# Sorting the first eleven row tiles on their own, moving the key extraction behind a product sum, and filling gather slots early in a sparse graph-attention kernel

## The chip, the cores and the metric

The kernel runs on one core of one Trainium2 chip. The metric is device time in microseconds (us) of one execution. TensorE is called PE below, VectorE DVE, ScalarE ACT, GpSimd POOL, and SyncE, which only issues DMAs, SP.

## What is computed

```python
h = jnp.maximum(_layernorm(x, axis=-1), 0.0)          # x: 2708 x 1024
q = h @ W_q.T + b_q ; k = h @ W_k.T + b_k ; v = h @ W_v.T + b_v
z = scale * (q @ k.T)                                  # 2708 x 2708
spare_z = z * adj                                      # adj: 0/1, density 0.0014771
spare_z = jnp.where(spare_z == 0.0, -10000.0, spare_z)
out = jax.nn.softmax(spare_z, axis=1) @ v
return x + jax.nn.relu(out)
```

A row of `adj` has about four ones. So only a few scores of a row count, and the kernel gathers those rows of h instead of forming the 2708 x 2708 matrix.

## The kernel before

**Tiling.** Rows are taken 128 at a time: 22 tiles, the last of 20 rows. The weights of q and k are multiplied into one matrix M at the start (until about 106 us), so that a query row times M is compared with rows of h directly. Tiles 0 to 10 are "early" (`EARLY = 11`), 11 to 21 "late".

**Search.** Each adjacency tile is loaded by SP. ACT sums it (`counted`, step letter p), and DVE finds the positions of the ones in four parts of a row by four `FIND_INDEX8` (`edges`, step letter f; e is p and f together). At the last tile of a batch of four (`BATCHES`), `edges` also turns the positions into sorted keys, by 18 small DVE instructions (lines 322 to 331). 

**Sort.** Rows are sorted by their number of ones, the early and the late rows each among themselves, so that a tile of sorted rows needs few gather slots. `counts` (L567) makes a one-hot table `hot` by counts; `sort` (L589) sums it by two matmuls (`ps_in`, `ps_all`) and makes positions `pos_i`; `put` scatters the 22 tiles of the table `tab` into DRAM by indirect DMAs issued on POOL, and `reload` brings them back in sorted order as `ptab`. The order on POOL is written out by hand in `sort`: late tiles put, early 0 to 3 put, late reload, early 4 and 5 put, first query rows of late tiles gathered (`first_rows`), early 6 to 10 put, early reload.

**Units.** PE's main work is 20 units, and each makes two row tiles times a 1024 x 1024 matrix by seven products of halves instead of eight. Units 0 to 4 are the queries of tiles 0 to 9, in natural order; then `single_query` makes tile 10; units 5 to 9 are the sorted late tiles 11 to 20; units 10 to 19 are outputs, and tile `alone` (11, the last of `order`) follows by itself. `multiply` (L917) runs one unit. Each block is four matmuls of 128x128 by 128x512 (eight instructions in the trace). Its blocks in order are s2, a12, s4, s3, then the next unit's first two (`opened`: a11 and s1), then a22. Between them `after(0)` to `after(6)` issue whatever else belongs there; `steps_at` (L692) lists, by unit and position, the search and normalisation steps. The operands s1 to s4 are DVE differences of transposed halves (L645; s2 and s4 on POOL in units 1 to 3), and the sums `q` (L963, L966) read product banks that PE wants back.

**Attention.** `attention` is a generator that DVE works through between units, from unit 5 on: for each sorted tile `scores` (L782) multiplies gathered rows `g` with the query rows `pq`, ACT makes exponentials (`w`, L798), `sums` (L835) adds the weighted rows into `u`, which goes to `u_dram`. Slots for gathered rows come from `free`: eleven tiles `g` and two parts of M. `fill` issues gathers (L524) while there are wanted rows and free slots. Slots 0 to 7 first hold the weight of v and its differences (`ts_of_wv`, unit 4).

**Order.** DVE keeps program order to the end of the last unit, ACT until unit 5, POOL until `pooled.close()` in `after(2)` of unit 3. PE, SP and the rest are ordered when the program is built, by a scheduler with a model of the times.

Of the kernel before, what the change touches and what calls it, by code (L numbers as in the profile page):

```python
# [18 lines left out]
P = 128  # L19
# [38 lines left out]
def tile_preln_masked_attention(  # L58
# [43 lines left out]
    tab_dram = [dram.tile([N, TW], FT, name=f"tab_dram{i}") for i in range(2)]  # L102
# [167 lines left out]
    def follow(steps):  # L270

        for step in steps.split():
            first, *only = step[1:].split(".")
            first, *last = first.split("-")
            first = int(first)
# [35 lines left out]
    def edges(t):  # L311

        a, n = loaded(t)
        first_t, last_t = next(b for b in BATCHES if b[0] <= t <= b[1])
        G = last_t - first_t + 1
# [3 lines left out]
        for g in range(PARTS):  # L319
            nc.vector.max_index(at[:n, t - first_t, g, :], ones[:n, 0:8], a[:n, g, :])  # L320
        if t == last_t:
# [219 lines left out]
    def put(lo, hi, puts):  # L541

        for t, (t0, n) in tiles_of(lo, hi):
            put = nc.gpsimd.indirect_dma_start(  # L544
                out=tab_dram[lo >= EARLY][:, :], out_offset=bass.IndirectOffsetOnAxis(ap=pos_i[:n, t:t + 1], axis=0),
                in_=tab[:n, t, :], in_offset=None)
            for other in puts:
                tc.declare_no_dep(put.ins, other.ins, reason="rows of a permutation")
            puts.append(put)

    def reload(lo, hi, puts):

        full = min(hi, FULL)
        loads = [nc.gpsimd.dma_start(ptab[:, lo:full, :],
                                     tab_dram[lo >= EARLY][lo * P:full * P, :].rearrange("(t p) w -> p t w", p=P))]
        if hi > FULL:
            loads.append(nc.gpsimd.dma_start(ptab[:REST, FULL, :], tab_dram[1][FULL * P:, :]))
        for load in loads:
            for put in puts:
# [5 lines left out]
    sorting, asked = [], []  # L565

    def counts():  # L567


        s1 = row_tile("sort")  # L570
        s2 = work.tile([P, D], FT, tag="hT", name="hot", bufs=2)
        sorting.extend((s1, s2))
        found = s1[:, 0:NT * SLOTS].rearrange("p (t s) -> p t s", s=SLOTS)
        nc.vector.tensor_scalar(found, keys, 0.0, None, op0=ALU.is_gt)
        nc.vector.tensor_reduce(bad, found, AX.X, ALU.add)
        nc.vector.tensor_copy(tab[:, :, SLOTS + 1:SLOTS + 2], bad.unsqueeze(2))
        nc.vector.tensor_sub(deg, bad, past)
        nc.vector.tensor_scalar_max(deg, deg, -1.0)

        W = ND * NT  # L580
        hot = s2[:, 0:W]
        for lo, hi in parts:
            n = hi - lo
            nc.vector.tensor_tensor(hot[:, ND * lo:ND * hi].rearrange("p (d t) -> p d t", d=ND),
                                    deg[:, lo:hi].unsqueeze(1).to_broadcast([P, ND, n]),
                                    down.unsqueeze(2).to_broadcast([P, ND, n]), op=ALU.is_equal)
        nc.vector.tensor_scalar(tab.bitcast(U32)[:, :, 0:SLOTS], keys, -1.0, float(N), op0=ALU.mult, op1=ALU.add)

    def sort():  # L589

        s1, s2 = sorting
        W = ND * NT
# [12 lines left out]
        for lo, hi in parts:  # L605
            nc.vector.tensor_reduce(deg[:, lo:hi], run[:, ND * lo:ND * hi].rearrange("p (d t) -> p t d", d=ND),
                                    AX.X, ALU.add)
# [19 lines left out]
        with tc.issue_after(back.ins):  # L627
            for t in sorted(owed):
                owe(t)
        return placed  # L630
# [42 lines left out]
    def natural_rows(n):  # L673
# [18 lines left out]
    steps_at = {(0, 0): "s4-5 e9", (0, 1): "r4 +0 +1 +2 f10", (0, 3): "p10 f11", (0, 4): "a4 p11", (0, 5): "h4 +3 s6-7 e12",  # L692
# [6 lines left out]
    def searched():  # L699
# [11 lines left out]
        with tc.issue_after(asked[0].ins):  # L711
            for i in range(8, HIGH):
                nc.gpsimd.memset(slots[i], 0.0)
        assert len(adj_loads) == NT
        free.extend(slots + [M.rearrange("p i j (a c) w -> p i j a (c w)", a=2)[:, 0, 1, a, :] for a in range(2)])
# [200 lines left out]

    def multiply(n, results, after):  # L917
# [20 lines left out]
        if n != FIRST - 1:  # L938
            opened(n + 1)
# [132 lines left out]
    def single_query():  # L1072
# [4 lines left out]
        add_block(X, single[0], M[:, 0, 0])  # L1077
        first = small("p_single")
        nc.scalar.copy(first, X)
# [14 lines left out]
    for n, unit in enumerate(units):  # L1094
# [10 lines left out]
        def after(i):  # L1105
            if (n, i) == (3, 2):
                pooled.close()
                counts()
            if (n, i) == (3, 3):
                with tc.issue_after(products[-1].ins):  # L1110
                    placed.append(sort())
            if (n, i) in ((4, 1), (4, 2)):
                ts_of_wv(2 * i - 2, 2 * i)
            if n == FIRST - 1 and i == 6:
# [31 lines left out]
            if (n, i) == (3, 4):  # L1146
                searched()
            if n == last_q - 1 and i == 4:
# [13 lines left out]
    while alone not in done:  # L1162
        advance(1.0)
# [38 lines left out]
    r, = load_rows(("o", alone))  # L1202
    uT = turned(r, "alone")
    X, Z = banks_for(bp_sb)
    add_block(X, uT[:, 0:4, :], M[:, 0, 0])
    p1 = small("p1")
    nc.scalar.copy(p1, X)
# [190 lines left out]
```

## Time and profile before

| | us |
|---|---|
| runs of the kernel | 671.61, 672.36, 674.16 (median 672.36) |
| the profiled execution's own time | 671.25 |
| its span, first to last instruction | 669.5 |
| PE busy in the span | 653.4 |
| DVE, ACT, POOL busy | 518.4, 266.2, 403.1 |
| DMA bytes, mean rate | 194.29 MB, 290 GB/s |
| first matmul of the M stage | 5.35 |
| first block of unit 0 | 108.59 |
| pair of sort matmuls | 203.57 |
| first score on DVE | 272.05 |
| last matmul ends, about | 660.8 |

Busy time of matmuls is taken from modelled ends, since they are pipelined. So in what follows the distance from the start of one block to the start of the next is used. It is 3.43 us in an undisturbed block of eight instructions, and 0.87 us for eight transposes.

### The profile page before, as it was taken

What the parts mean: (1) busy time and instruction counts of PE and PEld (TensorE: products, weight loads), DVE (VectorE), ACT (ScalarE), POOL (GpSimd) and SP (SyncE); (2) the same over time, 40 slices, a digit from 0 to 9 for tenths busy, and PEclk for the clock granted to TensorE, in tenths of its full rate; (3) what the DMA queues carried; (4) which work ended last, traced back from release to release, by engine and by line L of the source; (5) the groups of instructions that cost most, each with busy time, mean ns of one, the idle gap of its engine ahead of it and who ended that gap; (6) DMA issues with size and microseconds to landing.
All of it is one profiled execution on the core that took longest, in us unless ns stands there. A gap on an engine that the chain in (4) does not pass through costs nothing.

```text
span 669.5 us, 6372 instructions
## 1 busy us (share of the span) xinstructions
PE 653.4 (98%) x1764; PEld 332.4 (50%) x1764; DVE 518.4 (77%) x998; ACT 266.2 (40%) x399; POOL 403.1 (60%) x397
## 2 busy tenths in 40 slices
PE   7999999999999999999999999999999999999994
PEld 4777776444444444444444444444444444444441
DVE  5999879999589402799988899798788989989201
ACT  3467985855844212232242231432332433322220
POOL 2559991585513778676666366574674877872342
PEclk9999999999999999999999999999999999999998
DMA  8997989699566877799999999998997899794653
GB/s 344 407 360 262 368 302 374 235 372 352 204 218 227 279 242 229 270 373 348 326 340 352 403 411 386 293 306 247 333 294 191 235 304 356 212 284 141 175 136 117
DMA packets 62452, 194.29 MB, mean 290 GB/s; under 512 B 9721, under 2 KB 10073, under 8 KB 61514
## 3 DMA queue, kind: packets, MB, share of 16 engines
q0 software_dynamic: 34608, 109.77, 50.0%
q1 hardware_dynamic: 26794, 80.89, 32.5%
q10 hardware_dynamic: 1008, 3.15, 1.2%
q8 instruction: 16, 0.26, 0.2%
q14 instruction: 26, 0.21, 0.1%
HBM read 161.38 MB, written 45.46 MB: 309 GB/s over the span
## 4 chain that ended last, share of the span: by engine, by line
PE 83%; DVE 6%; issue 4%; DMA 3%; POOL 2%; ACT 1%; POOLq 0%; DVEq 0%
PE ps L898 37%; PE psy L898 26%; PE ps_y L397 6%; PE ps_x L397 5%; PE pt L338 4%; PE ps_z L397 4%; DVE junk L782 2%; DVE u L835 2%; DMA g<-h_dram,tab 2%; POOL g L524 1%; DMA out_dram<-y,tab 1%; DVE s L645 1%; DMA wlow<-in_wk_dram 1%; ACT a L641 0%; ACT u L827 0%
## 5 line engine op out<-in xcount | busy, mean ns | idle before, releaser
L524 POOL DMA_INDIRECT g<-h_dram,tab x106 | 129.9, 1226 | 46.7 <-issue 23.4
L898 PE MATMUL psy<-wlow,s 128*128 128x512 f32 x320 | 144.2, 593 | 1.3 <-ACT u L927 1.3
L898 PE MATMUL ps<-M,a 128*128 128x512 f32 x320 | 144.1, 593 | 0.1
L782 DVE SCALAR_TENSOR_TENSOR junk<-g,pq 128x1024 uint8<-128x1024 f32 x94 | 115.1, 1225 | 14.7 <-DMA pq<-q_dram,tab 12.6
L835 DVE SCALAR_TENSOR_TENSOR u<-g,coef,u 128x1024 f32<-128x1024 f32 x78 | 100.0, 1282 | 7.9 <-ACT u L827 4.9
L898 PEld LDWEIGHTS psy<-wlow,s 128*128 128x128 f32 x320 | 59.2, 190 | 69.4 <-issue 66.8
L898 PEld LDWEIGHTS ps<-M,a 128*128 128x128 f32 x320 | 59.3, 190 | 68.0 <-issue 67.2
L320 DVE FIND_INDEX8 at<-ones,adj 128x8 uint32<-128x685 f32 (+1 forms) x88 | 74.4, 865 | 0.0
L898 PE MATMUL psy<-wlow,a 128*128 128x512 f32 x160 | 72.3, 595 | 1.2 <-DVE q L963 0.8
L898 PE MATMUL ps<-wlow,s 128*128 128x512 f32 x160 | 72.1, 593 | 0.8 <-DVE s L645 0.7
L898 PE MATMUL ps<-M,s 128*128 128x512 f32 x160 | 71.9, 592 | 0.0
L981 POOL DMA_INDIRECT y<-in_x_dram,tab x21 | 37.0, 1763 | 49.2 <-ACT y L996 23.1
L309 ACT ACTIVATE sized<-adj 128x2708 uint8<-128x2708 f32 (+1 forms) x22 | 54.2, 2465 | 4.2 <-DMA adj<-in_adj_dram 4.1
L898 PEld LDWEIGHTS psy<-wlow,a 128*128 128x128 f32 x160 | 30.0, 190 | 40.3 <-issue 34.2
L898 PEld LDWEIGHTS ps<-wlow,s 128*128 128x128 f32 x160 | 30.2, 190 | 39.8 <-issue 37.1
L898 PEld LDWEIGHTS ps<-M,s 128*128 128x128 f32 x160 | 30.3, 190 | 37.6 <-issue 37.1
L257 POOL TENSOR_TENSOR hsum<-hsum,x 128x1024 f32<-128x1024 f32 (+1 forms) x17 | 40.3, 2371 | 0.4
L645 DVE TENSOR_TENSOR s<-a,pt 128x512 f32<-128x512 f32 x40 | 25.6, 682 | 17.5 <-ACT a L641 9.2
L641 ACT COPY a<-pt 128x512 f32<-128x512 f32 x60 | 33.2, 593 | 4.9 <-issue 3.3
L544 POOL DMA_INDIRECT tab_dram<-tab,pos_i x22 | 22.6, 1028 | 20.2 <-DVE pos_i L608 13.8
L827 ACT ACTIVATE u<-g,coef 128x1024 f32<-128x1024 f32 x16 | 18.4, 1148 | 34.8 <-DVE coef L826 26.8
L736 POOL DMA_INDIRECT out_dram<-y,tab x21 | 25.1, 1195 | 8.9 <-issue 5.8
(230 smaller groups left out, 871.6 us busy)
## 6 DMA issues: line engine op xcount, KB each, us to landing
adj<-in_adj_dram SPq DMA_DIRECT2D x21, 1354.0 KB
x<-in_x_dram SPq DMA_DIRECT2D x21, 512.0 KB
h_dram<-x POOLq DMA_DIRECT2D x21, 512.0 KB
u_dram<-u POOLq DMA_DIRECT2D x15, 512.0 KB
or<-u_dram SPq DMA_DIRECT2D x15, 512.0 KB
q_late<-q SPq DMA_DIRECT2D x10, 512.0 KB
pq<-q_late POOLq DMA_DIRECT2D x10, 512.0 KB
g<-in_wv_dram SPq DMA_DIRECT2D x16, 256.0 KB
```

The lines of the kernel that those rows point to most:

```text
L257: nc.gpsimd.tensor_add(hsum[:n], hsum[:n], xt[:n])
L309: nc.scalar.activation(sized[:n], a[:n, :, :PW], AF.Abs, accum_out=total[:n, t:t + 1])
L320: nc.vector.max_index(at[:n, t - first_t, g, :], ones[:n, 0:8], a[:n, g, :])
L338: nc.tensor.transpose(pt[:, c, :], xt[:, k * P:(k + 1) * P], ident)
L397: mm = nc.tensor.matmul(bank, a_tile(o + H * a[0], a[1], i), b(o), start=first and o == 0, stop=(o == H - 1), skip_group_check=True)
L524: return nc.gpsimd.indirect_dma_start(out=dst, out_offset=None, in_=src, in_offset=off, bounds_check=N - 1, oob_is_err=False)
L641: nc.scalar.copy(ops[name], bank)
L645: step = (eng or nc.vector).tensor_tensor(ops[name], a, b, op=op)
L782: chained(lambda: nc.vector.scalar_tensor_tensor(junk, g_of[t][s], 1.0, tq[t], op0=ALU.mult, op1=ALU.mult, accum_out=zall[:, t, s:s + 1]))
L835: chained(lambda: nc.vector.scalar_tensor_tensor(u, g_of[t][s], coef[:, at[t][s]:at[t][s] + 1], u, op0=ALU.mult, op1=ALU.add))
L898: mm = nc.tensor.matmul(bank, a[:, c, :], b[:, c, :], start=False, stop=(c == 3), skip_group_check=True)
L981: return nc.gpsimd.indirect_dma_start(out=y[:n], out_offset=None, in_=x, in_offset=off, compute_op=ALU.add)
```

## The change

Five things change.

1. **Search of tile 11.** `edges` is split into `found` (the four index searches, letter i) and `listed` (the keys of a finished batch, letter j). In unit 0 position 3 becomes `p10 i11`, and the keys of the batch 8 to 11 are made at position 4, behind the sum q of the s4 block and behind the operands s1 and s3 of unit 1.
2. **Two sorts.** `counts` and `sort` take a range of tiles. The early range is counted at position (2,1) and sorted at (2,4); the search of tile 19 goes from (2,4) to (2,5), behind the other sum q of unit 2; the early tiles are put and reloaded after it (step w), and POOL's fixed order ends there. The late range is counted and sorted in unit 3, where all 22 tiles were, and `entered` puts and reloads it, gathers the first query rows and adds the owed rows.
3. **Gather slots.** Three tiles are asked for instead of two. The two parts of M and slots 8 to 10 are handed out first, at (4,2); slots 0 to 7 follow where the first entries were filled before, at (4,6). The zeroing of slots 8 to 10 no longer waits for the first query rows.
4. **First block of tile 10.** It goes between s3 and a22 of unit 4 (`between`, `one_started`), where other units have `opened`; it stood behind a22.
5. **Tile `alone`.** Its `u` is loaded and transposed at position 1 of the last unit, and its first block goes ahead of a22 of that unit. Its other three blocks stay at the end.

```diff
+    def put(lo, hi):
+        before_them = puts[lo >= EARLY]
...
-    def counts():
-        s1 = row_tile("sort")
-        s2 = work.tile([P, D], FT, tag="hT", name="hot", bufs=2)
...
+    def counts(lo, hi):
+        n = hi - lo
+        s1, s2 = [work.tile([P, D], FT, tag="hT", name=name, bufs=2) for name in ("sort", "hot")]
...
-        placed = nc.vector.tensor_copy(pos_i, deg)
-        late, early = [], []
-        put(EARLY, NT, late)
-        with tc.issue_after(late[-1].ins):
-            put(0, 4, early)
-        with tc.issue_after(early[-1].ins):
-            back = reload(EARLY, NT, late)
-        with tc.issue_after(back.ins):
-            put(4, 6, early)
-        with tc.issue_after(early[-1].ins):
-            rows = first_rows(0)
+        return nc.vector.tensor_copy(pos_i[:, lo:hi], deg[:, lo:hi])
+
+    def entered():
+        with tc.issue_after(put(EARLY, NT).ins):
+            late = reload(EARLY, NT)
+        with tc.issue_after(late.ins):
+            rows = first_rows(0)
         with tc.issue_after(rows.ins):
             rows = first_rows(1)
-        asked.append(rows)
-        with tc.issue_after(rows.ins):
-            put(6, EARLY, early)
-        with tc.issue_after(early[-1].ins):
-            back = reload(0, EARLY, early)
...
+            elif step == "c":
+                counts(0, EARLY)
+            elif step == "o":
+                sort(0, EARLY)
+            elif step == "w":
+                pooled.close()
+                with tc.issue_after(put(0, EARLY).ins):
+                    back.append(reload(0, EARLY))
             else:
                 if step[0] == "e":
                     counted(first)
-                edges(first)
+                if step[0] != "j":
+                    found(first)
+                if step[0] != "i":
+                    listed(first)
...
-    steps_at = {(0, 0): "s4-5 e9", (0, 1): "r4 +0 +1 +2 f10", (0, 3): "p10 f11", (0, 4): "a4 p11", (0, 5): "h4 +3 s6-7 e12",
+    steps_at = {(0, 0): "s4-5 e9", (0, 1): "r4 +0 +1 +2 f10", (0, 3): "p10 i11", (0, 4): "j11 a4 p11", (0, 5): "h4 +3 s6-7 e12",
...
-                (1, 6): "f16", (2, 1): "f17", (2, 2): "p16 a8", (2, 3): "h8 f18 p17",
-                (2, 4): "s10 f19 p18", (2, 5): "r10", (2, 6): "f20 f21 a10 k10 p19", (3, 2): "p20", (3, 3): "p21"}
+                (1, 6): "f16", (2, 1): "f17 c", (2, 2): "p16 a8", (2, 3): "h8 f18 p17",
+                (2, 4): "o s10 p18", (2, 5): "f19 r10 w", (2, 6): "f20 f21 a10 k10 p19", (3, 2): "p20", (3, 3): "p21"}
...
-        free.extend(slots + [M.rearrange("p i j (a c) w -> p i j a (c w)", a=2)[:, 0, 1, a, :] for a in range(2)])
+        free.extend([M.rearrange("p i j (a c) w -> p i j a (c w)", a=2)[:, 0, 1, a, :] for a in range(2)] + slots[8:])
...
-        for t in order[:2]:
+        for t in order[:3]:
             ask(t)
+        fill()
+        yield 0.0
...
+        free.extend(slots[:8])
         fill()
         yield 0.0
...
+    def between(n):
+        if n == FIRST - 1:
+            single["first"] = one_started(single["banks"], single[0])
+        elif n == len(units) - 1:
+            single["first"] = one_started(single["banks"], single["turned"][:, 0:4, :])
+        else:
+            opened(n + 1)
+
+    def one_started(banks, a):
+        X, Z = banks
+        add_block(X, a, M[:, 0, 0])
+        first = small("p_single")
+        nc.scalar.copy(first, X)
+        return first
...
-        if n != FIRST - 1:
-            opened(n + 1)
+        between(n)
...
             if (n, i) == (3, 2):
-                pooled.close()
-                counts()
+                counts(EARLY, NT)
             if (n, i) == (3, 3):
                 with tc.issue_after(products[-1].ins):
-                    placed.append(sort())
+                    placed.append(sort(EARLY, NT))
+                entered()
...
-            if n == FIRST - 1 and i == 6:
+            if (n, i) == (FIRST - 1, 2):
+                next(stream)
+            if (n, i) == (FIRST - 1, 6):
...
+            if nxt is None and i == 1:
+                while alone not in done:
+                    advance(1.0)
+                r, = load_rows(("o", alone))
+                single["turned"] = turned(r, "alone")
+            if nxt is None and i == 3:
+                single["banks"] = banks_for(bp_sb)
...
-    while alone not in done:
-        advance(1.0)
```

More of the change, by code (lines that the diff above doesn't have):

```diff
@@ L101, in tile_preln_masked_attention @@
     parts = [(0, EARLY), (EARLY, NT)]
-    tab_dram = [dram.tile([N, TW], FT, name=f"tab_dram{i}") for i in range(2)]
+    tab_dram = [dram.tile([size, TW], FT, name=f"tab_dram{i}") for i, size in enumerate((EARLY * P, N - EARLY * P))]
     tail_dram = dram.tile([1, D], FT, name="tail_dram")
@@ L320, in edges, with listed @@
             nc.vector.max_index(at[:n, t - first_t, g, :], ones[:n, 0:8], a[:n, g, :])
+    def listed(t):
+        first_t, last_t = next(b for b in BATCHES if b[0] <= t <= b[1])
+        G = last_t - first_t + 1
+        n = tiles[t][1]
+        at = seen[-1]
         if t == last_t:
@@ L539, in tiles_of @@
         return list(enumerate(tiles))[lo:hi]
-    def put(lo, hi, puts):
+    puts = ([], [])
+    def put(lo, hi):
+        before_them = puts[lo >= EARLY]
         for t, (t0, n) in tiles_of(lo, hi):
@@ L563, in reload, with sort @@
         return loads[-1]
[L565 to L589 removed]
+    sorting, back = [], []
+    def counts(lo, hi):
+        n = hi - lo
+        s1, s2 = [work.tile([P, D], FT, tag="hT", name=name, bufs=2) for name in ("sort", "hot")]
+        sorting[:] = s1, s2
+        found = s1[:, 0:n * SLOTS].rearrange("p (t s) -> p t s", s=SLOTS)
+        nc.vector.tensor_scalar(found, keys[:, lo:hi], 0.0, None, op0=ALU.is_gt)
+        nc.vector.tensor_reduce(bad[:, lo:hi], found, AX.X, ALU.add)
+        nc.vector.tensor_copy(tab[:, lo:hi, SLOTS + 1:SLOTS + 2], bad[:, lo:hi].unsqueeze(2))
+        nc.vector.tensor_sub(deg[:, lo:hi], bad[:, lo:hi], past[:, lo:hi])
+        nc.vector.tensor_scalar_max(deg[:, lo:hi], deg[:, lo:hi], -1.0)
+        nc.vector.tensor_tensor(s2[:, 0:ND * n].rearrange("p (d t) -> p d t", d=ND),
+                                deg[:, lo:hi].unsqueeze(1).to_broadcast([P, ND, n]),
+                                down.unsqueeze(2).to_broadcast([P, ND, n]), op=ALU.is_equal)
+        nc.vector.tensor_scalar(tab.bitcast(U32)[:, lo:hi, 0:SLOTS], keys[:, lo:hi], -1.0, float(N), op0=ALU.mult, op1=ALU.add)
+    def sort(lo, hi):
         s1, s2 = sorting
[L592 removed]
+        W = ND * (hi - lo)
         hot = s2[:, 0:W]
@@ L1201, in tile_preln_masked_attention @@
     tail(NT - 1)
[L1202 to L1207, printed above, removed]
+    uT, (X, Z), p1 = single["turned"], single["banks"], single["first"]
     add_block(Z, uT[:, 0:4, :], T[:, 0])
```

37 lines of the change are left out of this document (15 added, 22 removed).

## The prediction

> **What bounds the kernel now.** I read the page's busy times first, then the waits of PE, then PE's timeline, and last what stood on the waited-for engine.
>
> ```profile
> PE 653.4 (98%) x1764; PEld 332.4 (50%) x1764; DVE 518.4 (77%) x998; ACT 266.2 (40%) x399; POOL 403.1 (60%) x397
> ```
>
> PE is busy from end to end, at a mean granted clock of 0.997. The change takes no product away, so it can win only PE's gaps. At the ends nothing of it acts: M starts as before, and from the last matmul's end (660.8) a DVE sum, a scatter and the closing waits run to 669.5. The gaps between are few:
>
> ```profile
> PE psy L898 <- ACT u L927: 1.3, 1, 1.3
> PE psy L898 <- DVE q L963: 0.8, 1, 0.8
> PE ps L898 <- DVE s L645: 0.7, 1, 0.7
> ...
> PE ps_in L595 <- DVE hot L584: 0.5, 1, 0.5
> ```
>
> Ends of matmuls are modelled, so I size each gap by starts (PE's timeline: start, us, instructions):
>
> ```profile
> 130.39 3.60 PE L898 MATMUL ps<-M,a 128*128 128x512 f32 x8
> 134.71 3.70 PE L898 MATMUL ps<-wlow,s 128*128 128x512 f32 x8 [0.73 <-DVE s L645]
> ...
> 186.38 3.60 PE L898 MATMUL ps<-wlow,s 128*128 128x512 f32 x8
> 190.74 3.70 PE L898 MATMUL psy<-wlow,a 128*128 128x512 f32 x8 [0.76 <-DVE q L963]
> ...
> 199.46 3.60 PE L898 MATMUL ps<-M,a 128*128 128x512 f32 x8
> 203.57 0.90 PE L595 MATMUL ps_in<-hot,before 128*128 128x396 f32 x2 [0.52 <-DVE hot L584]
> ...
> 271.64 3.60 PE L898 MATMUL ps<-M,s 128*128 128x512 f32 x8
> 276.58 3.70 PE L898 MATMUL psy<-wlow,s 128*128 128x512 f32 x8 [1.35 <-ACT u L927]
> 280.12 3.60 PE L898 MATMUL ps<-M,a 128*128 128x512 f32 x8
> 283.80 3.70 PE L898 MATMUL ps<-wlow,s 128*128 128x512 f32 x8
> 287.57 3.70 PE L898 MATMUL psy<-wlow,a 128*128 128x512 f32 x8
> ```
>
> An undisturbed block takes 3.43 from start to start, and the first block behind a gap 0.11 more. So the gaps cost: A at 134.71, 4.32 - 3.43 + 0.11 = 1.0; B at 190.74, 4.36 - 3.43 + 0.11 = 1.04; C at 203.57, 4.11 - 3.43 = 0.68; D from 276.58 to 287.57, 1.51 + 0.11 + 0.25 + 0.34 + 0.11 = 2.32; E, a wait for the sum L991 at 573.53, 0.62. Sum 5.7: the most that this change can win.
>
> **Keys behind the sum (gap A).** DVE has no idle time from 106 to 153. Behind tile 11's search it makes the keys of a batch, 130.19 to 133.37 (3.2), then the sum q (L966), and only at 133.98 the operands s1 and s3 that PE waits for. Afterwards s1 and s3 follow the sum directly, at 130.75; their inputs are there (ACT's copy of a22 ends at 128.15). PE's s1 block then starts at 133.82 without a wait. The keys now stand ahead of the sum L963, which ends at 135.8 as before, since the work ahead of it is the same; its taker, a22, starts at 137.25. **Gain 1.0.**
>
> **Early sort in unit 2 (gap B).** DVE's sum for a22 stood behind tile 19's search and a batch of keys (183.4 to 190.0). Both move behind it. The early `counts` adds seven DVE instructions: before, over 22 tiles, they took 0.34, 0.52, 0.19, 0.17, 0.18, 0.64 and 0.34 (2.4 in all); over 11 tiles about 1.6. They lie in DVE's idle time 168.6 to 173.1 (a wait for ACT, 4.58); without this cover they would cost unit 2's operands 1.6. The early `sort` adds seven more: 0.56, 0.98, 0.57, 0.57, 0.57, 0.46, 0.18 at double width, some 2.6 at this one. It waits for its two matmuls, and behind it on DVE wait tile 10's statistics (1.5), the sum (0.6), tile 19. PE, 1.0 earlier by gap A, starts the matmuls at 178.5 and s3 at 179.3; DVE is through with the sort near 182.5 and with the sum near 184.7. PE wants it at 189.6. So gap B goes (1.04) and a pair of matmuls is paid: 203.57 to 204.98 was 1.41 for 396 columns, so about 0.7 for 198. **Gain 0.35.**
>
> **Late sort (gap C).** DVE's search of tiles 20 and 21 began at 192.15, after 1.47 of waiting for the adjacency load. The moved batch ends near 191.3, so it stays under that wait. The load goes out when ACT has summed tile 17, and ACT may be up to 1.0 earlier; I take 0.5. From 201.35 `hot` took 2.08; eleven tiles should take 1.4. `hot` is ready at 201.35 - 0.5 + 1.4 = 202.25, the pair starts at 202.4 and takes 0.7: unit 3 goes on at 203.1 instead of 204.98. This is **1.9 for A, B and C together** (with the load at its old time 1.4, a full 1.0 earlier 2.3).
>
> **Early gathers (gap D).** DVE's first score waited to 272.05:
>
> ```profile
> 272.05 1.22 DVE L782 SCALAR_TENSOR_TENSOR junk<-g,pq 128x1024 uint8<-128x1024 f32 x1 [12.62 <-DMA pq<-q_dram,tab]
> ```
>
> The early table was reloaded last (issued at 251.63), six gathers and two qr rows went ahead of pq (265.95) on POOL's queue, and the DMA engines were 0.9 busy from 258 on, at 1.6 to 1.8 per 512 KB. ACT, in the order laid down for it, held the exponentials (idle 10.3 for L782) ahead of the copy u (L927) that PE needed. Now eleven puts (1.3 apart, 14.3) and the reload run from about 187 to 205 on a POOL that idled until 210.97 but for one store; late puts follow from 208 to 222 and query rows are gathered near 229 instead of 237.81. Five gathers, 2.6 MB, can go before 255, where the DMA share was 0.66 and 0.26 in the last two stretches of 5. Tile 10's store (255.81, some 2 earlier now) then frees pq: it lands between 260 and 264 against 270 on the moved scale. Gap D needs the first three scores done by 272 there, that is, a start before 268. **Gain 2.3**, bounds 0 and 2.32.
>
> **Tile `alone`.** PE has as many blocks as before. Its transposes (0.87) only filled the wait of a22 for the sum L991 (642.51 to 643.42), which its first block fills now. **Gain 0**, and a risk: the transposes are asked for at the last unit's start, 628.64.
>
> ```profile
> 622.31 0.60 POOL L844 DMA_DIRECT2D u_dram<-u  x1
> ...
> 628.36 0.34 SPq L1048 DMA_DIRECT2D or<-u_dram  x1
> 630.00:631.00 1.00, 1.00 (x4) 0.49 (x3) 0.00 (x0) 0.06 (x1) 1.00 (x1) 1.00 0.91 373
> ```
>
> The store takes 5.45 from 622.91 to release its load, whose bytes move until about 631.2 (the last row is a stretch of 1 us: DMA share 0.91, 373 GB/s). All of it shifts with PE. Transposes put first would wait 2.6; behind the s2 block (632.07), nothing. [...]
>
> Gap E stays: DVE meets PE at 511.36 (it waits 1.28 for it) and is late again by its own work at 573, so it shifts with PE (bounds 0 to 0.62).
>
> **Sum.** 1.9 + 2.3 = **4.2**, taken from the profiled execution of 671.25: 667.0 (span 665.3). The median of the runs, 672.36, lies 1.1 above it; on that scale **668.2**, with 1.4 to 2.3 plus 2.0 to 2.9 (a little of E) giving 667.2 to 669.0.
>
> **Rivals.**
> - *The load of `alone` is late.* PE takes the transposes first, waits 2.6 and pays 0.3 around it: gain 1.3, 671.1. For it: they stand first in program order. Against: before, the scheduler put them into a gap, and a modelled late load would again.
> - *The pq wait stays.* POOL sends the second five gathers ahead of pq, 5 x 1.8 = 9 of queue, and the first score starts at 270: gain 1.9 alone, 670.5. For it: that is what POOL did before. Against: idle DMA time before 255.
> - *The early sort stalls DVE: slower.* If its matmuls are put behind the blocks a11 and s1 that unit 2 opens instead of ahead of s3, DVE stands until 190.3; sort, statistics and sum end at 195.0, a22 starts at 195.1 instead of 189.6, tiles 19 to 21 end near 210.6, the late pair starts at 212.1 and unit 3 goes on at 212.8, 7.9 late; less D, 5.5: 677.9. It decides once the pair is later than about 186. For it: nothing ties these matmuls to a place. Against: their input is ready at 170 and they come first in program order.
>
> **How the numbers follow.** The forecast has 0.47, the late load 0.2, the pq wait 0.12, the slow sort 0.15, and 0.06 is for a wait that I don't see. Half a per cent, 3.4, is about what a measurement of this kernel can tell from no change; the line lies at 669.0. Faster: 0.47 and a little of the rest, 0.5. Within: late load and pq wait, 0.32. Slower: 0.18. The range 666.0 to 672.2 takes in both middle cases, leaving the slow sort out.
>
> **What would show it.** In PE's waits the lines of L645, of L963 and of L927 are gone, and that of `hot` is at most 0.5; the early `pos_i` is written near 183; the first score starts before 266 with `pq` gathered by 259; the last unit's s2 block starts 3.43 after a22's. A wait of PE for `or` or its copies, or for the early `ps_in`, makes the prediction wrong; so does a DVE wait of over 3 us in unit 2.

## The result, and the profile after

The changed kernel takes **678.58 us** (median of 11 runs, 674.90 to 680.21) against 672.36 before (11 runs, 670.75 to 675.90). The ratio is **1.0081, 95% interval 1.0059 to 1.0104**: slower by 0.8 per cent, where the prediction had 668.2 and a range of 666.0 to 672.2. The profiled execution took 678.58, its span 676.8, 7.3 more than the 669.5 before.

PE's waits in the changed kernel (who waited for whom: us in total, times, longest):

```profile
PE psy L904 <- DVE q L985: 2.7, 1, 2.7
PE pt L355 <- DMA or<-u_dram: 2.6, 1, 2.6
PE ps_in L611 <- ACT a L645: 2.0, 1, 2.0
...
PE psy L904 <- DVE p L1013: 0.4, 1, 0.4
```

The waits that were to go are gone from their places: the one for s1 and s3 (L645 before), the one for the sum in unit 2 (L963 before) and the one for the copy u (L927 before). Three longer ones have come. One is for the same sum (L985 now), but in unit 1. One is for `or`, the row of `alone`. One stands ahead of the late pair, where at most 0.5 was to be left. PE's timeline shows where (start, us, instructions):

```profile
130.01 3.60 PE L904 MATMUL ps<-M,a 128*128 128x512 f32 x8
133.45 3.60 PE L904 MATMUL ps<-wlow,s 128*128 128x512 f32 x8
137.12 3.70 PE L904 MATMUL psy<-wlow,a 128*128 128x512 f32 x8
...
165.86 5.40 PE L904 MATMUL psy<-wlow,a 128*128 128x512 f32 x8 [2.69 <-DVE q L985]
171.09 1.04 PE L355 MATMUL pt<-ident,x 128*128 128x128 f32 x8
...
183.15 0.50 PE L611 MATMUL ps_in<-hot,before 128*128 128x198 f32 x2
183.48 0.50 PE L613 MATMUL ps_all<-hot,ones 128*128 128x198 f32 x2
183.82 3.60 PE L904 MATMUL psy<-wlow,s 128*128 128x512 f32 x8
...
208.36 0.57 PE L611 MATMUL ps_in<-hot,before 128*128 128x198 f32 x2 [2.03 <-ACT a L645]
...
633.87 1.70 PE L355 MATMUL pt<-ident,or 128*128 128x128 f32 x8 [2.57 <-DMA or<-u_dram]
635.36 3.83 PE L904 MATMUL psy<-wlow,s 128*128 128x512 f32 x6
639.03 3.60 PE L904 MATMUL ps<-M,a 128*128 128x512 f32 x8
```

The reader should set each start against the same block before. That gives a running balance of how late PE is:

| reached | after - before | what came in between |
|---|---|---|
| first block of unit 0 | -0.38 | differs before the change acts |
| a22 of unit 0 | -1.13 | gap A gone |
| first transposes behind unit 1's a22 | +3.62 | waits 2.69 for the sum, then the block takes 1.7 too long |
| s3 of unit 2 | +4.30 | the early pair, 0.67 |
| a22 of unit 2 | +3.38 | gap B gone |
| s4 of unit 3 | +4.12 | waits 2.03 ahead of the late pair |
| a22 of unit 5 (287.57 before) | +1.73 | gap D gone |
| last unit, a12 (632.07 before) | +6.96 | waits 2.57 for the row of `alone`, six matmuls and transposes too slow |
| last blocks of `alone` (653.72 before) | +6.13 | its transposes are no longer here |
| end of the span | +7.3 | the end behind PE is 1.2 longer |

Behind two of the waits PE also ran slower. By stretches of 1 us (PE, PEld, DVE, ACT, POOL busy; then the granted clock, DMA share, GB/s):

```profile
165.00:166.00 1.00, 0.14 (x1) 0.14 (x2) 0.98 (x4) 0.00 (x0) 0.00 (x0) 1.00 0.98 357
166.00:167.00 1.00, 1.00 (x2) 0.38 (x3) 1.00 (x3) 0.00 (x0) 0.00 (x0) 0.75 0.99 385
167.00:168.00 1.00, 1.00 (x3) 0.35 (x2) 1.00 (x3) 0.00 (x0) 0.00 (x0) 0.50 0.56 222
168.00:169.00 1.00, 1.00 (x3) 0.48 (x2) 1.00 (x3) 0.00 (x0) 0.00 (x0) 0.50 0.08 33
169.00:170.00 1.00, 1.00 (x3) 0.48 (x2) 1.00 (x5) 0.00 (x0) 0.00 (x0) 0.54 0.03 14
```

The clock is at half for 0.50 + 1 + 1 + 0.92 = 3.42 us, which costs 1.7. From 634 to 638 it is the same (0.57, 0.50, 0.50, 0.73: 3.40 at half). Whether the clock falls differs from run to run of one kernel, and the times with it: six of twelve runs of alone_keys_again (below) took 669.14 to 669.59 at a mean granted clock of 0.996, the other six 671.14 to 671.87 at 0.993 to 0.995. The store of the row of `alone` and the load that PE waits for there, from the queues of POOL and SP in the changed kernel:

```profile
623.86 0.60 POOL L847 DMA_DIRECT2D u_dram<-u  x1
...
630.08 0.34 SPq L1070 DMA_DIRECT2D or<-u_dram  x1
```

On DVE two things had changed their length, and one load came late (changed kernel, DVE's timeline):

```profile
131.56 0.98 DVE L342 TENSOR_TENSOR cand<-first,at 128x128 f32<-128x128 f32 x1
132.58 1.31 DVE L343 SCALAR_TENSOR_TENSOR cand<-at,cand 128x128 f32<-128x128 uint32 x1
...
149.52 0.09 DVE L330 MATCH_VALUE_LOAD at<-ones,adj 128x8 f32 x1 [2.52 <-DMA adj<-in_adj_dram]
...
184.42 2.51 DVE L617 TENSOR_TENSOR_SCAN sort<-sort 128x198 f32<-128x198 f32 x1
```

The same instructions in the kernel before:

```profile
130.19 0.29 DVE L325 TENSOR_TENSOR cand<-first,at 128x128 f32<-128x128 f32 x1
130.52 0.29 DVE L326 SCALAR_TENSOR_TENSOR cand<-at,cand 128x128 f32<-128x128 uint32 x1
...
206.72 0.98 DVE L601 TENSOR_TENSOR_SCAN sort<-sort 128x396 f32<-128x396 f32 x1
```

The two key instructions took 0.29 each before. The scan took 0.98 for 396 columns and now takes 2.51 for half as many. Tile 14's adjacency was searched without a wait in the trace of the kernel before. POOL's timeline in the changed kernel, beside the key instructions:

```profile
131.13 1.27 POOL L649 TENSOR_TENSOR s<-s,a 128x512 f32<-128x512 f32 x1 [1.32 <-DVE s L649]
132.47 1.26 POOL L649 TENSOR_TENSOR s<-a,s 128x512 f32<-128x512 f32 x1
133.69 0.66 POOL L255 DMA_DIRECT2D h_dram<-x  x1
134.37 2.37 POOL L257 TENSOR_TENSOR hsum<-hsum,x 128x1024 f32<-128x1024 f32 x1
136.67 0.58 POOL L255 DMA_DIRECT2D h_dram<-x  x1
```

And in the kernel before:

```profile
134.74 1.27 POOL L645 TENSOR_TENSOR s<-s,a 128x512 f32<-128x512 f32 x1 [4.61 <-DVE s L645]
...
137.30 0.66 POOL L255 DMA_DIRECT2D h_dram<-x  x1
...
140.28 0.57 POOL L255 DMA_DIRECT2D h_dram<-x  x1
```

There POOL idled until 134.74, waiting for s1 and s3, and its two stores of h went out at 137.30 and 140.28. So the moved keys now run beside the very work that they used to hold back, and the stores (512 KB each) start 3.6 us earlier.

### The profile page after: what moved, and what is told of

It is laid out like the page before. It is cut to its first block, busy times and chain, and to the rows that moved or that the text cites. A ratio compares the mean times of both kernels' runs of the same rounds, so it can differ in the third digit from the quotient of the medians.

```text
span 676.8 us, 6390 instructions
## 1 busy us (share of the span) xinstructions
PE 655.5 (97%) x1768; PEld 334.8 (49%) x1768; DVE 525.7 (78%) x1010; ACT 266.3 (39%) x399; POOL 402.1 (59%) x397
## 4 chain that ended last, share of the span: by engine, by line
PE 74%; DVE 10%; DMA 7%; issue 4%; ACT 3%; POOL 1%; POOLq 0%; ACTq 0%; SPq 0%; DVEq 0%
PE ps L904 32%; PE psy L904 23%; PE ps_y L414 6%; PE ps_x L414 4%; PE ps_z L414 4%; PE pt L355 4%; DMA adj<-in_adj_dram 3%; DVE u L838 2%; DVE at L330 2%; DVE junk L785 1%; DVE s L649 1%; DMA y<-in_x_dram,tab 1%; ACT sized L320 1%; DMA u_dram<-u 1%; DMA out_dram<-y,tab 1%
## 5 line engine op out<-in xcount | busy, mean ns | idle before, releaser
L541 POOL DMA_INDIRECT g<-h_dram,tab x104 | 124.6, 1198 | 51.3 <-issue 22.8
L785 DVE SCALAR_TENSOR_TENSOR junk<-g,pq 128x1024 uint8<-128x1024 f32 x92 | 112.6, 1223 | 2.0
L904 PE MATMUL psy<-wlow,a 128*128 128x512 f32 x160 | 73.9, 606 | 3.1 <-DVE q L985 2.7
L649 DVE TENSOR_TENSOR s<-a,pt 128x512 f32<-128x512 f32 x40 | 25.6, 680 | 17.2 <-ACT a L645 9.7
L543 POOL DMA_INDIRECT pq<-q_dram,tab x11 | 15.5, 1411 | 33.2 <-DVE junk L785 21.2
L645 ACT COPY a<-pt 128x512 f32<-128x512 f32 x60 | 33.2, 593 | 4.2 <-PE pt L355 4.2
L541 POOL DMA_INDIRECT M<-h_dram,tab x20 | 25.9, 1293 | 11.1 <-issue 4.9
```

The lines of the kernel that those rows point to most:

```text
L541: return nc.gpsimd.indirect_dma_start(out=dst, out_offset=None, in_=src, in_offset=off, bounds_check=N - 1, oob_is_err=False)
L645: nc.scalar.copy(ops[name], bank)
L649: step = (eng or nc.vector).tensor_tensor(ops[name], a, b, op=op)
L785: chained(lambda: nc.vector.scalar_tensor_tensor(junk, g_of[t][s], 1.0, tq[t], op0=ALU.mult, op1=ALU.mult, accum_out=zall[:, t, s:s + 1]))
L904: mm = nc.tensor.matmul(bank, a[:, c, :], b[:, c, :], start=False, stop=(c == 3), skip_group_check=True)
```

## The experiments

Ratios are to the kernel before on the same chip, with 95% intervals. The letters of the steps in the edits, beside those named above: s is the statistics of a tile on DVE, r the eight small POOL instructions that make its scale, a the scaling on ACT, h the stores of two tiles of h and their adds into `hsum` on POOL, k the stores alone, with the adds left owed, and + such an owed add. Dots in the code stand for lines or steps that are not shown.

### Which parts cost

**alone_at_end**: tile `alone` put back to the end, the rest of the change kept.

```diff
-            if nxt is None and i == 1:
...
-                r, = load_rows(("o", alone))
-                single["turned"] = turned(r, "alone")
...
-            single["first"] = one_started(single["banks"], single["turned"][:, 0:4, :])
...
```

> The changed kernel with tile alone left at the end (load, transposes and first block behind the last unit, as before). Theory: in the changed kernel's trace the last unit loses 4.5 us on PE (2.6 of waiting for the load of alone, 1.75 of matmuls at a lower granted clock behind that wait, some transposes), and 1.2 more pass between the last matmul and the end, since the last unit's results reach POOL later. So this kernel is 5.0 to 5.9 us faster than the changed one, near 673, and its granted clock in the last unit is 1.0. Rival: the wait is paid anyway, because PE then waits for the sum L991 in the same unit; the gain is under 1.5 us.

672.39 (669.44 to 674.18), ratio 0.9994 [0.9977, 1.0010]. The early start of `alone` costs 6.2 by the medians (5.8 by the ratios).

**keys_back**: the keys of tile 11's batch back to position (0, 3).

```diff
-    ... (0, 3): "p10 i11", (0, 4): "j11 a4 p11", ...
+    ... (0, 3): "p10 f11", (0, 4): "a4 p11", ...
```

> The changed kernel with the keys of tiles 8 to 11 made in their old place, ahead of the sum q. Theory 1: moving them let POOL store normalised rows 3.6 us earlier and SP ask for x and adjacency tiles 3 us earlier, and that traffic made adjacency tile 14 land 4 us late; here tile 14's search has no wait, a22 of unit 1 starts within 0.5 us of its place in the kernel before, gap A (1.0 us) is back, and the kernel is 3 to 4 us faster than the changed one. Theory 2: the late landing is chance of one execution (the DMA rate was 277 to 337 GB/s around 130 us against 393 to 428); here it comes or stays away as it likes, and over all runs the kernel is 1 us slower than the changed one or the same.

675.89 (673.89 to 676.90), ratio 1.0049 [1.0031, 1.0067]: 2.7 below the changed kernel by the medians, 2.2 by the ratios, where theory 1 had put 3 to 4. Gap A is back (a wait of 1.2 for s L649), and PE's wait in unit 1 is gone. DVE still waits 2.16 for tile 14's adjacency, against theory 1, but its search starts at 147.42 instead of 149.52.

**r10_first**: the eight POOL instructions of r10 ahead of the early puts, which the prediction had assumed.

```diff
...
-                with tc.issue_after(put(0, EARLY).ins):
+                with tc.issue_after(rooted[-1].ins):
+                    last_put = put(0, EARLY)
+                with tc.issue_after(last_put.ins):
...
```

> The changed kernel with the eleven early puts tied behind the eight small POOL instructions of tile 10's scale (r10). In the changed kernel POOL took them in turn with the puts, so they ended at 203.6 us instead of about 192, ACT's step for tile 10 waited 5.3 us and held the copies behind it, and ps_in waited until 208.36. Theory 1: the one-hot table of the late sort was ready at 208.22 by DVE's own lateness, so the late ps_in starts no earlier: a gain under 0.4 us. Theory 2: ACT was what held it: the wait of 2.0 us goes, gain 1.5 to 2.1 us.

677.22 (673.67 to 679.46), ratio 1.0065 [1.0041, 1.0090]. The wait ahead of the late pair is 2.1 as before and only names another releaser, `hot` instead of the copy behind a10. DVE held it too.

**alone_keys**: both undone.

> The changed kernel without the early alone tile and without the moved keys. If the two losses are independent, its gain over the changed kernel is the sum of the two single ones: 8 to 10 us if tile 14's lateness comes from the moved keys (near 669.5, faster than the kernel before by 3), 4 to 5 us if that is chance.

669.47 (669.14 to 671.33), ratio 0.9956 [0.9939, 0.9972]. What is left of the change, the two sorts and the early gathers, gains. A repeat on another chip (alone_keys_again) gave 670.37, 0.9966 [0.9949, 0.9983].

### Tile alone

**alone_later**: the changed kernel; the load stays at position 1 of the last unit, the transposes are asked for at position 4.

```diff
-                r, = load_rows(("o", alone))
-                single["turned"] = turned(r, "alone")
+                single["rows"], = load_rows(("o", alone))
+            if nxt is None and i == 4:
+                single["turned"] = turned(single["rows"], "alone")
```

> The changed kernel, but in the last unit the transposes of tile alone's row are asked for behind the fifth product (i = 4) instead of the second; the load stays where it is. It splits the 6.2 us that tile alone cost into the wait for its row and the rest. Theory 1 (the wait): the changed kernel lost 2.57 waiting for `or`, and the six matmuls behind it took 3.83 where 6/8 of 3.43 is 2.57; without the wait the last unit's blocks start 3.43 apart and the time is 3 to 5 us below the changed kernel's 678.6, 674 to 675.5; the late results of the last unit on POOL's queue (1.2 at the end) stay. Theory 2 (it is the queue at the end, since the first block of alone stands ahead of the last unit's results): no more than 1.5 below the changed kernel.

673.04 (669.84 to 674.45), ratio 1.0008 [0.9990, 1.0025]: 5.5 below the changed kernel by the medians, 4.9 by the ratios. PE's timeline of it:

```profile
635.97 3.60 PE L904 MATMUL ps<-M,s 128*128 128x512 f32 x8
639.40 1.04 PE L355 MATMUL pt<-ident,or 128*128 128x128 f32 x8
640.28 3.60 PE L904 MATMUL psy<-wlow,s 128*128 128x512 f32 x8
```

The same transposes, three blocks later, wait for nothing and take 1.04, and the block behind them takes its 3.60. **later_keys** (the same with the keys put back) tells whether the queue at the end costs as well:

> The changed kernel with the keys put back and tile alone's transposes asked for behind the fifth product: all the rest of the change stays. The prediction gave tile alone's early start a gain of 0 if its load doesn't hold PE. Theory 1 (the wait was all there is to it): within 0.7 of alone_keys. Theory 2 (GpSimd's queue at the end costs 1.2, since the last unit's results come one block later): 0.8 to 1.5 above alone_keys.

670.31 (669.93 to 672.48), ratio 0.9979 [0.9961, 0.9998], against 670.37, ratio 0.9966, for alone_keys on the same chip: equal by the medians, 0.9 slower by the ratios. So the wait and its clock were most of it. The early start of `alone` wins nothing, and a cost of up to 0.9 at the end (theory 2) is not ruled out.

### The late pair

**alone_keys_r10** (alone_keys with r10 first, the edit above):

> Tile alone and the keys put back (669.5 so far), and on GpSimd's queue the root of tile 10 (r10) ahead of the early puts, as the prediction assumed. Theory 1 (DVE's own lateness holds the late pair of matmuls): the wait of 2.1 for the copy behind a10 becomes one for `hot`, about as long, time within 1 of 669.5. Theory 2 (r10 between the puts holds it): the wait falls below 0.7 and the time is 667.5 to 668.5.

670.83 (668.87 to 672.03), ratio 0.9974 [0.9957, 0.9991]; PE's wait ahead of the late pair is 2.07, as with r10 between the puts. That is theory 1's wait; the time is 1.4 above the first median of alone_keys and 0.5 above the second, where at most 1 was put. **alone_keys_k8** moves two POOL adds away from beside the early sort's scan; **alone_keys_s10** moves the scan instead, by putting tile 10's statistics ahead of the sort:

```diff
-    ... (2, 3): "h8 f18 p17", ...
+    ... (2, 3): "k8 f18 p17", ...      # alone_keys_k8: the stores, the adds later
-    ... (2, 4): "o s10 p18", ...
+    ... (2, 4): "s10 o p18", ...       # alone_keys_s10
```

> alone_keys with one edit: GpSimd's two adds of tiles 8 and 9 into hsum, one of which runs beside the early sort's scan, are made later, among the gathers. Theory 1 (the scan is slow because GpSimd adds beside it): the scan takes 0.6 instead of 2.5, `hot` of the late tiles is 1.9 earlier; since r10 still stands between the puts, ACT's copy behind a10 holds the late pair as before and the wait stays 1.5 to 2.0, so the time is within 1 of alone_keys. Theory 2 (a scan of 198 columns is slow by itself here): it stays at 2.5.

> alone_keys with one edit: in unit 2 tile 10's statistics stand ahead of the early sort on DVE. They have one SBUF input and took 1.28 beside GpSimd before; so the scan starts 1.5 later, overlaps GpSimd's add by 0.6 instead of 2.1, and r10 is ready before the puts, which follow it in GpSimd's order. Theory 1 (scan beside the add, and r10 between the puts, together hold the late pair): scan 1.0 to 1.4, `hot` ready 1 to 1.5 earlier, the wait of 2.05 falls below 1.2, no drop of the granted clock behind it, time 1 to 3 below alone_keys. Theory 2 (something else, such as the adjacency load, holds DVE): the wait stays at 1.8 or more and the time within 0.5.

668.00 (667.27 to 669.29), ratio 0.9933 [0.9907, 0.9959], and 668.03 (667.50 to 671.30), 0.9938 [0.9916, 0.9959]. From DVE's and PE's timelines of alone_keys_k8:

```profile
180.60 0.57 DVE L617 TENSOR_TENSOR_SCAN sort<-sort 128x198 f32<-128x198 f32 x1
...
202.31 0.37 DVE L600 TENSOR_TENSOR hot<-deg,down 128x198 f32<-128x198 f32 x1
```

```profile
202.82 0.57 PE L611 MATMUL ps_in<-hot,before 128*128 128x198 f32 x2 [0.31 <-DVE hot L600]
```

PE's timeline of alone_keys:

```profile
204.90 0.62 PE L611 MATMUL ps_in<-hot,before 128*128 128x198 f32 x2 [2.05 <-ACT a L645]
```

The scan is back at 0.57 and the late pair starts at 202.82 with a wait of 0.31, where alone_keys had 204.90 and 2.05. With the scan moved it overlaps POOL's add by some 0.8 and takes 1.19, and the wait is 0.47. The wait that I thought r10 shared in is the scan's alone: in alone_keys_k8 r10 still stands between the puts. My expectation of "within 1 of alone_keys" was wrong there: it is 2.4 faster on the same chip. Part of this is PE's clock. In alone_keys it was 0.50 for 3.42 us behind this wait, and the block of 3.60 behind the pair took 4.96; in the repeat that block took 5.01, in the traces of these two kernels 3.60.

### The moved keys

**b_keys**: the kernel before with the moved keys alone.

> The kernel before with the moved keys alone (batch made behind the sum L963's place: tile 11 only searched at (0, 3), keys at (0, 4)). Forecast in the prediction: gain 1.0, gap A gone and nothing else. Theory 1 (the keys slow down beside GpSimd): the two instructions with two SBUF inputs that take 0.29 each before now take about 1.0 and 1.3 beside GpSimd's s2 and s4, the sum for a22 of unit 1 is late again and PE waits there 1 to 3 us: time 0 to +3 against before. Theory 2 (the loss needs the other parts, the earlier stores or the early sort): gap A gone, no wait in unit 1, time 0.5 to 1.0 below before.

673.45 (671.30 to 678.70), ratio 1.0035 [1.0013, 1.0057]. The loss needs no other part of the change. PE waits 2.02 in unit 1, as theory 1 had it; whether its cause holds is for the next kernels. **alone_keys5**: `alone` at the end, and the batch one step later, behind the sum for a22.

> Tile alone put back to the end, and the moved keys one step later still: at the head of (0, 5), behind the sum for a22 and past GpSimd's s2 and s4. Against alone_at_end (keys at (0, 4), 672.4) and alone_keys (keys where they were, 669.5). Theory 1 (GpSimd beside it is what the move costs): the two instructions take 0.29 each again, gap A stays away, PE's wait for the sum in unit 1 is below 0.5, time 668 to 669.5. Theory 2 (any keys behind a22's sum push tile 12's search and the adjacency loads back, and unit 1's sum with them): the wait in unit 1 is 1 us or more and the time 671 to 673.

673.02 (670.99 to 674.82), ratio 1.0011 [0.9992, 1.0031], with a wait in unit 1 of 3.6. These are the numbers of theory 2, but POOL was still beside the keys (busy for 3.90 of the 4 us from 132 to 136; the two instructions took 0.39 and 1.31), so theory 1 wasn't put to the test. In its trace the stores of h go out at 133.74 and 136.73, and DVE waits 1.38 and 2.40 for the adjacency of tiles 13 and 14. The next kernels stand on **mended_base** (alone_keys_k8 once more), which repeats at 668.24, ratio 0.9951 [0.9937, 0.9964]. **keys4_k8** has the keys where the change puts them, **keys11_k8** ahead of tile 14's search, and **all_mended** is keys11_k8 with the early start of `alone` as in alone_later.

```diff
-    ... (0, 3): "p10 f11", (0, 4): "a4 p11", ...     (1, 1): "f14", ...       # mended_base
+    ... (0, 3): "p10 i11", (0, 4): "j11 a4 p11", ... (1, 1): "f14", ...       # keys4_k8
+    ... (0, 3): "p10 i11", (0, 4): "a4 p11", ...     (1, 1): "j11 f14", ...   # keys11_k8
```

> mended_base with the keys at the place that the change gives them, behind the sum and beside GpSimd's s2 and s4. Both theories: the wait for the sum in unit 1 is back, 1.4 to 2.7, and the time 1.5 to 3.5 above mended_base.

> mended_base with the keys later still, ahead of tile 14's search (step (1, 1)), when GpSimd has made s2, s4 and two of its three adds. Theory 1 (GpSimd beside the keys is the cost): the first instruction takes at most 0.6 and the second 0.29, the batch lies where DVE would wait for the adjacency load, gap A is gone, PE's wait for the sum of unit 1 is below 0.5, time 0 to 1 below mended_base. Theory 2 (a later batch takes DVE's slack, wherever it stands): the wait in unit 1 is 1 or more and the time is 1 or more above mended_base.

> The whole change with three faults undone: keys ahead of tile 14's search, the two adds moved from beside the scan, tile alone's transposes asked for behind the last unit's fifth product (its early start stays). Expected the time of keys11_k8 within 0.8, and 9 to 12 below the changed kernel's 678.6.

keys4_k8: 670.80, ratio 0.9980 [0.9965, 0.9995], 2.6 above mended_base with a wait of 2.35 in unit 1, as expected. keys11_k8: 671.84, 1.0004 [0.9991, 1.0018]. all_mended: 671.20, 0.9998 [0.9984, 1.0012], close to keys11_k8, but 7.4 below the changed kernel where 9 to 12 was expected. DVE's timeline of keys11_k8, then PE's:

```profile
143.59 0.09 DVE L330 MATCH_VALUE_LOAD at<-ones,adj 128x8 f32 x1 [4.88 <-DMA adj<-in_adj_dram]
...
146.97 0.27 DVE L342 TENSOR_TENSOR cand<-first,at 128x128 f32<-128x128 f32 x1
147.28 0.29 DVE L343 SCALAR_TENSOR_TENSOR cand<-at,cand 128x128 f32<-128x128 uint32 x1
```

```profile
166.38 5.40 PE L904 MATMUL psy<-wlow,a 128*128 128x512 f32 x8 [3.04 <-DVE q L983]
```

My theory fell here, and the time and the wait are those of theory 2. The instructions are short again, POOL is not beside them, and PE waits longer: DVE stands 4.88 for tile 13's adjacency load, and the batch comes behind that. What all kernels with gap A closed share is a POOL that is 3 us ahead. It then issues its two stores of h, and frees the buffer for the next x load, 3 us earlier, into DMA engines that are full (share 0.96 to 1.04 in each 4 us from 132 to 148 in mended_base, keys4_k8 and keys11_k8). Two kernels delay one of these each, from keys4_k8:

```diff
-    ... (0, 5): "h4 +3 s6-7 e12", (0, 6): "r6 f13", ...
+    ... (0, 5): "+3 s6-7 e12",    (0, 6): "r6 h4 f13", ...   # keys4_h4: the stores later
+    ... (0, 5): "h4 s6-7 e12",    (0, 6): "r6 +3 f13", ...   # keys4_3late: the x load later
```

> keys4_k8 with GpSimd's two stores of h in unit 0 (and their adds) moved behind the add of an owed tile and behind r6: the stores go out near 143 and 146 instead of 134.2 and 137.2; the x load behind that add goes out earlier still, near 137 instead of 142.6. Theory 1 (the earlier stores delay the adjacency load): tile 14's search starts at 147.5 or before, PE's wait in unit 1 falls from 2.4 to below 0.8, time 667.5 to 669.5. Theory 2 (the earlier x and adjacency loads delay it): the search starts at 149.5 or later, the wait stays at 2 or more, time 670.5 or more.

> keys4_k8 with the add of the owed tile moved behind r6 instead: the stores stay at 134.2 and 137.2, the x load and tile 15's adjacency load go out near 145 to 146, as in the kernel before. Theory 1 (the earlier stores): tile 14's search starts at 149.5 or later and the wait in unit 1 stays at 2 or more, time 670.5 or more. Theory 2 (the earlier x and adjacency loads): the search starts at 147.5 or before, the wait is below 0.8, time 667.5 to 669.5.

**keys4_h4: 666.73** (666.00 to 669.30), ratio **0.9928 [0.9910, 0.9946]**, the best of all. keys4_3late: 671.05 (667.84 to 672.63), 0.9979 [0.9963, 0.9995]. PE's waits of keys4_h4, its POOL timeline, and the start of tile 14's search on DVE; then the same start in keys4_3late, keys4_k8 and mended_base:

```profile
PE psy L904 <- DVE p L1011: 0.4, 1, 0.4
PE psy L904 <- DVE q L983: 0.3, 1, 0.3
```

```profile
142.93 0.66 POOL L255 DMA_DIRECT2D h_dram<-x  x1 [0.30 <-issue]
...
145.92 0.58 POOL L255 DMA_DIRECT2D h_dram<-x  x1
```

```profile
146.45 0.09 DVE L330 MATCH_VALUE_LOAD at<-ones,adj 128x8 f32 x1
```

```profile
150.45 0.09 DVE L330 MATCH_VALUE_LOAD at<-ones,adj 128x8 f32 x1 [3.04 <-DMA adj<-in_adj_dram]
```

```profile
149.72 0.09 DVE L330 MATCH_VALUE_LOAD at<-ones,adj 128x8 f32 x1 [2.58 <-DMA adj<-in_adj_dram]
```

```profile
147.07 0.09 DVE L330 MATCH_VALUE_LOAD at<-ones,adj 128x8 f32 x1 [1.72 <-DMA adj<-in_adj_dram]
```

With the stores 9 us later DVE waits for no adjacency load (tile 14's search ends at 149.84, when s1 begins). And that although the x load, free at 136.06, now stands ahead of tile 14's load on SP's queue, so that this goes out at 136.56 instead of 133.28. The 0.3 left is unit 0's. With the x load late and the stores early the wait is 3.04 and PE's 2.80. Of the two, the stores are the cause; how the DMA engines share their time between the queues the traces don't show. The two key instructions still take 0.98 and 1.31 in keys4_h4, and that costs no more than the 0.3. So neither theory 1 of keys11_k8 (POOL beside the keys) nor its theory 2 (a later batch takes DVE's slack, wherever it stands) is the main cost.

One trace can't size the delay. When the load of tile 14 lands differs by 2 us between traces with the keys in their old place: it is there by 145.29 in the kernel before and at 147.42 in keys_back. The kernel before, alone_keys and alone_keys_r10 search tile 14 without a wait, keys_back waits 2.16 and mended_base 1.72, and PE waits in unit 1 in none of them. The latest of these five starts that search at 147.42, the earliest of the eight with the keys at (0, 4) or (0, 5) and the first store before 135 at 148.35 (alone_later). The cost is read from the run times: 0.9979 with the early stores and 0.9928 with the late ones, on one chip. No run delays the stores with the keys in their old place, so what late stores would win by themselves is open.

## Why the prediction was wrong

**Keys behind the sum: 1.0 was to be gained, 1.6 to 2.9 was lost** (by the medians: b_keys against the kernel before 1.6, keys4_k8 against mended_base 2.6, the changed kernel against keys_back 2.7, alone_at_end against alone_keys 2.9). Gap A went, but a22 of unit 0 starts only 0.75 earlier against unit 0's first block: the sum that was to end at 135.8 ended at 137.07, behind the longer key instructions. The step that failed is "the work ahead of it is the same" and with it the list of what the move releases. I followed PE's side of s1 and s3 only. POOL waits for them too, and behind them stand its DMAs: the h stores went out 3.6 earlier, tile 14's adjacency came late, and DVE, which had idled 1.18 in unit 1 before, was late for the sum of unit 1, where PE waited 2.69. The longer key instructions are a second slip, with little price (0.3 in keys4_h4).

**Early sort.** Gap B is gone, and the pair costs 0.67 where 0.7 was put. It starts at 183.15, directly ahead of s3, so the rival of the stalled sort is out. Mis-sized was "some 2.6" for DVE: in alone_keys it is 4.8 (180.53 to 185.30), because the scan takes 2.52 where half of 0.98 was put; in alone_keys_k8, without POOL beside the scan, it is 2.8 (180.20 to 183.03).

**Late sort.** `hot` at 202.25 and the pair at 202.4 were worked out; the changed kernel, 3.4 late by then, has a wait of 2.0. The scan had taken 2 us of the DVE time on which `hot` depends. In alone_keys_k8 the pair starts at 202.82, so the step's working holds once the scan's time does. That r10 would go ahead of the puts was also wrong, and made no difference.

**Early gathers.** Gap D is gone and 2.2 of 2.3 are won (PE is 3.93 late at the start of unit 5's first product block, 272.13, and 1.73 at its a22). pq landed later than I put it: POOL issued its gather at 266.44, once tile 10's store had landed, and the first score started at 270.79, 266.9 without PE's 3.9. So the sign that I had set, a start before 266, was missed, and the bound that decided, a start before 268, held by 1.1.

**Tile `alone`.** Its row in the list of rivals came true: the wait is 2.57 where 2.6 was worked out from the store and load of before. The store was issued at 623.86, the load followed at 630.08. The sign that was to make the prediction wrong, a wait of PE for `or`, is in the trace. What failed is the argument against this rival, that the scheduler would put the transposes into a gap: it put them behind the first quarter of the s2 block, with the load still under way. What times its model gave them the record doesn't show. And the price was short: 2.6 + 0.3 became 4.9 to 6.2. Of the rest 1.7 is the clock, which fell to half for 3.4 us behind the wait, and up to 1.2 the longer end behind PE.

**Gap E** stayed (0.4), as said. **The sum**: 4.2 of gain was close to what the parts are worth where nothing is held up. alone_keys_k8 gains 3.9 on its chip without the moved keys, and keys4_h4 gains 5.2 with them. Part of the latter is luck: in its trace 0.6 of the 5.2 stands already at unit 0's first block (107.96 against 108.59), ahead of anything that the change touches, which leaves some 4.6. The loss lies in three side effects: the load of `alone` (about 6), the stores (about 3) and the scan (about 2, in part through the clock).

## What to carry to other kernels

When a step moves off the bottleneck's path, list what it releases on every other engine, DMAs too, and ask which transfer shares the DMA engines with them; here a store that nobody waited for decided the time of a load (tile 14's search at 149.72 with the stores early, in keys4_k8, and at 146.45 with them late, in keys4_h4). Price an instruction by who runs beside it at its new place: here the two key instructions and the scan on DVE lasted until POOL's operand or add was done (0.29 became 0.98 to 1.36, 0.57 became 2.51). Work whose input comes from a late load should be asked for behind work that covers the load, since an order by modelled times need not do it.

## What was not expected of the hardware

**A wait can cost more than its length.** In the units PE's clock was 0.50 for 3.40 to 3.42 us behind the waits of 2.05 (alone_keys), 2.57 and 2.69 (the changed kernel), and 1.00 behind those of 2.03 (the changed kernel's late pair) and 2.72 (r10_first). For the other waits the blocks behind them tell. Behind 3.04 (keys11_k8) and 3.56 (alone_keys5) the block took 5.40 and 5.39, as behind the 2.69. Behind 2.05 (b_keys), 2.80 (keys4_3late), and 1.75 (all_mended) or less it took no more than 3.70, and behind 2.51 (r10_first) six matmuls took 2.74, where the changed kernel's took 3.83. So waits of 2.0 to 2.8 went either way, two of 2.05 among them; what decides it the traces don't show.

**Two inputs in SBUF beside POOL.** Scan of 198 columns: 0.57 alone (alone_keys_k8), 1.19 beside the end of an add (alone_keys_s10), 2.51 beside a whole one (the changed kernel). The two key instructions: 0.29 alone (the kernel before), 0.98 to 1.36 beside what was left of one of POOL's operands or adds, and 0.39 for the first of them in alone_keys5. In each trace that shows both, the lengthened DVE instruction ends 0.14 to 0.44 behind POOL's: the first key instruction at 132.54 and POOL's s2 at 132.40, the scan at 186.93 and POOL's add at 186.49. So what it costs there is what is left of POOL's instruction. Beside POOL's small instructions of step r the key instructions took 0.29 as alone (158.03 and 158.36 in the kernel before). Statistics with one input took 1.28 beside an add (180.32 in the kernel before) and 1.28 without one (185.30 in alone_keys). What in an instruction makes the difference no run separates.
